# Layer 3's convolution on quarters of the array: sixteen strips in four groups, each product on half the rows and half the columns

## The chip, the cores and the metric

The kernel runs on one core of a Trainium2 chip. The metric is the device time of one execution in microseconds. TensorE is written PE in the profile, VectorE DVE, ScalarE ACT, GpSimd POOL and SyncE SP.

## What is computed

Sixteen samples of 16 channels, 256 x 256 pixels in float32, pass four residual layers. In each, the sample is normalised over pairs of channels, convolved, and added to what came in. Layer 0 is a circular 3x3 convolution, layer 1 a diagonal one of five taps, layer 2 works in the Fourier domain. Only layer 3 is changed:

```python
x_q = jnp.round(jnp.clip(x_cl / scale_input, -n, n))        # n = 127, one scale for the whole tensor
acc = lax.conv_general_dilated(x_q, w_hwio, window_strides=(1, 1), padding=((1, 1), (1, 1)), ...)
out = acc * (scale_input * scale_weight) + bias
...
x = x + _L3_conv_ref(_gn(x), L3_conv_weight_int8, L3_conv_scale_weight, L3_conv_bias)
```

Its input is quantized to whole numbers from -127 to 127, which bf16 holds exactly, convolved with a 3x3 kernel with zeros around the image, scaled and added to x.

## The kernel before

The layers run one after the other: layers 0 and 1 up to about 1270 us, the Fourier stages of layer 2 up to 4046 us, then layer 3 to the end. Between stages the data lie in DRAM: x2d after layer 1, x3d after layer 2.

Layer 3 is the last block of `layers` (from line 1206). An image is cut into S = 8 strips of R = 32 rows. Partition c * 8 + s holds channel c of strip s (`by_strip`, line 253), so a sample is one tile `xt` of [128, 32, 256] float32. A product contracts over all 128 partitions, that is over 16 channels and 8 strips at once. Its weights are a 128 x 128 matrix that is nonzero only where the strip of the input and that of the output agree (`strip_weights`, line 212, which multiplies the 16 x 16 taps with a table of strips). A tap that looks over a strip's edge reads the first or last row of the same tile with a second set of weights, 3 for above and 3 for below, that shifts by one strip; where there is no neighbour they are zero, which gives the padding.

For each sample b (line 1212) the block does this:

- Four chunks of RC = 8 rows: SyncE issues a load of 1 MB (line 1217) from x3d. ScalarE scales and shifts it into u (line 1219; a3 and b3 are the normalisation and the quantizing scale for each partition). VectorE rounds u in place by adding and subtracting a large constant (line 1220), and clips it into the bf16 tile q (line 1221), whose rows have 260 columns, 2 and 2 of them zero for the padding. Two such tiles take turns, `qs`.
- Sixteen tiles of two output rows, t = 1 to 15 and then 0 (`conv`, line 234): nine taps into one PSUM bank [128, 2, 256]. A tap is one product of 512 columns, or two of 256 where its rows lie on both sides of the strip's edge. Line 250 is the product.
- For each tile `done` (line 1223) lets ScalarE scale and shift the bank into o (line 1225), VectorE adds o to xt in place (`tt`, line 189), and after every fourth tile GpSimd issues a store of a chunk of 8 rows, 1 MB, to the output (line 1231).

The pools have 3 tiles of xt, 3 of u, 4 of o and 6 PSUM banks. No order is written by hand in this block: the scheduler of the tile framework puts each engine's instructions into a queue by data flow and its own estimates, and adds the semaphore waits. So loads and quantizing of sample b+1 are mixed with evictions of sample b on ScalarE and VectorE. SyncE issues loads only, and its load of a sample waits until the stores of the sample three before have landed. GpSimd in this block issues stores only. The weights `wt` and the zero columns of `qs` are made during layer 2 (lines 1160 to 1164).

Three other places matter for reading the trace. Line 1142 loads `ot`, 64 partitions a time, the two partition halves in turn, with runs of 1 KB; line 1149 loads `xt` of layer 2 on all 128 partitions with the same runs. In layers 0 and 1, line 370 loads x to 32 partitions a time, and line 466 stores x2d from 32 partitions a time. Line 412 is layer 0's product on column halves of the array.

Of the kernel before, what the change touches and what calls it, by code (L numbers as in the profile page):

```python
# [49 lines left out]
F32 = mybir.dt.float32  # L50
BF16 = mybir.dt.bfloat16
AF = mybir.ActivationFunctionType
ALU = mybir.AluOpType
AX = mybir.AxisListType
PSUM = bass.MemoryType.PSUM
DRAM = bass.MemoryType.DRAM

P = 128
C = 16
S = 8  # L60
R = 32
RC = 8
N = 256
NX = 129
NP = 4
# [6 lines left out]
def constants():  # L72

    n = np.arange(N)
    m = np.arange(128)
    even, odd = 2 * np.arange(64), 2 * np.arange(64) + 1
    fx = np.concatenate([[128], even, odd])
    fy = np.stack([np.concatenate([even, odd]), -np.concatenate([[128], even[1:], odd])], 1).reshape(-1)

    def cos(a, b):  # L80
        return np.cos(2.0 * np.pi * (np.outer(a, b) % N) / N)

    def sin(a, b):
# [12 lines left out]
    inv = np.stack([np.stack([np.concatenate([cos(even, m), v * cos([128], m), v * sin(even[1:], m)], 0),  # L96
                              np.concatenate([cos(odd, m), v * sin(odd, m)], 0)], 1) for v in (-1, 1)], 2)

    h = 0.5 / N**2
    last = np.stack([h * np.concatenate([cos([0], m), 2 * cos(even[1:], m), cos([128], m), -2 * sin(even[1:], m)], 0),  # L100
                     h * np.concatenate([2 * cos(odd, m), -2 * sin(odd, m)], 0)], 1)
    p = np.arange(P)[:, None]
    q = np.arange(P)[None, :]
    c16, c8 = np.arange(C)[None, :], np.arange(S)[None, :]
    s = p % S
    strip = np.stack([s == c8, (s + 1) % S == c8, (s - 1) % S == c8, s + 1 == c8, s - 1 == c8], 1)
# [8 lines left out]
    parts = {  # L115
        "y1": np.concatenate(y1, 1), "x1": np.concatenate(x1, 1), "x2": np.concatenate(x2, 1),
        "full": full, "inv": inv, "last": last, "alone": alone,
        "not0": 1.0 * (p > 0),
        "strip": strip,
        "chan": p // S == c16,  # L120
        "imag": 1.0 * (p % 2 == 1), "real": 1.0 * (p % 2 == 0),
        "group4": (p % 32 // 4 == q % 32 // 4) / 16.0,
        "first": p == 4 * c8,
        "mod": p % 8 == c8,


        "turn": np.stack([np.where(p < 64, 1.0, -1.0), np.where(p // 32 % 2 == 0, -1.0, 1.0),
                          1.0 * (p // 32 % 2 == 1), 1.0 * (p // 32 % 2 == 0)], 1),

        "turn_q": np.concatenate([np.where(im, sb, -sa), np.where(im, -sa, -sb)], 1),  # L130
        "vi": 1.0 * ((p // 64 == np.arange(16)[None, :] // 8) & (p % 8 == np.arange(16)[None, :] % 8)),
        "diag": p // NP % C == c16,
        "m1": np.diag(np.where(p[:, 0] < 64, 1.0, -1.0)) / (2 * N) ** 2,
        "m2": (p == (q + 64) % P) / (2 * N) ** 2,
        "eye": 1.0 * (p == q),
        "mean": np.full((P, P), 1.0 / P),
        "ones": np.ones((P, P)),
        "quarter": np.where(p < 64, 0.25, 0.0),
        "sign": np.where(p < 64, 1.0, -1.0),
        "nat": nat.reshape(128, 2),  # L140
    }
# [23 lines left out]
def layers(ctx, tc, x, w0, w1, w3, sw, bias, ty, tx, p1a, p1b, p1c, p2a, p2b, p2c, resa, resb,  # L165
           const, rows, out):
    nc = tc.nc
# [44 lines left out]
    def strip_weights(pool, src, taps, dtype, name, parts):  # L212
# [2 lines left out]
        raw = pool.tile([P, taps, C], F32, tag=f"{name}r", name=f"{name}r")  # L215
        nc.sync.dma_start(raw, src)
        n = sum(c for _, _, c, _ in parts)
        w = pool.tile([P, n, P], dtype, tag=name, name=name)
        for to, frm, count, m in parts:
            for i in range(count):  # L220
                tt(Q, w[:, to + i, :].rearrange("p (o s) -> p o s", s=S), bc(raw[:, frm + i, :], 2, S),
                   bc(strip[:, m, :], 1, C), MUL)
        return w

    def taps3x3(w, flip):

        taps = []
        for dy in (0, -1, 1):
            for dx in (0, -1, 1):
                ky, kx = (1 - dy, 1 - dx) if flip else (1 + dy, 1 + dx)  # L230
                far = None if dy == 0 else w[:, (9 if dy < 0 else 12) + kx, :]
                taps.append((dy, dx, w[:, 3 * ky + kx, :], far))
        return taps

    def conv(psum, v, taps, done):

        for t in (*range(1, R // 2), 0):
            ps = psum.tile([P, 2, N], F32, tag="ps_c", name="ps_c")
            work = []
            for dy, dx, near, far in taps:  # L240
                cols = slice(2 + dx, 2 + dx + N)
                r0 = 2 * t + dy
                if 0 <= r0 and r0 + 2 <= R:
                    work.append((ps, near, v[:, r0 : r0 + 2, cols]))
                    continue
                for r in range(2):
                    inside = 0 <= r0 + r < R
                    work.append((ps[:, r, :], near if inside else far, v[:, (r0 + r) % R, cols]))
            for i, (o, w, src) in enumerate(work):
                nc.tensor.matmul(o, lhsT=w, rhs=src, start=i == 0, stop=i == len(work) - 1)  # L250
            done(t, ps)

    def by_strip(d):
        return d.rearrange("c (s r) w -> (c s) r w", s=S)


    SL = 32
# [771 lines left out]
    qs = [last_.tile([P, R, 260], BF16, tag=f"q{k}", name=f"q{k}") for k in range(2)]  # L1029


    with ExitStack() as es:
# [97 lines left out]
        with tc.manual_schedule(engines={mybir.EngineType.PE}):  # L1130
            before = None
            exps = exponentials(0)
            for k in range(0, C, 2):
                for b in range(B):
# [23 lines left out]
                        along_x(*before)  # L1158
                    before = (b, k, zts, fs, exps[1], xt)
                    if k == C // 2 and b == 0:  # L1160
                        wt = strip_weights(last_, w3, 9, BF16, "wt3", [(0, 0, 9, 0), (9, 0, 3, 3), (12, 6, 3, 4)])
                        for q in qs:
                            Q.memset(q[:, :, 0:2], 0.0)
                            Q.memset(q[:, :, 258:260], 0.0)
                exps = coming
            along_x(*before)

# [35 lines left out]
        tt(V, so, so, top_all, MUL)  # L1203


    with ExitStack() as es:
        xp = es.enter_context(tc.tile_pool(name="e_x", bufs=3))
        up = es.enter_context(tc.tile_pool(name="e_u", bufs=3))
        rp = es.enter_context(tc.tile_pool(name="e_r", bufs=4))
        ps_c = es.enter_context(tc.tile_pool(name="e_ps", bufs=6, space=PSUM))  # L1210
        taps = taps3x3(wt, False)
        for b in range(B):
            xt = xp.tile([P, R, N], F32, tag="xt4", name=f"xt4_{b}")
            q = qs[b % 2]
            for r in range(0, R, RC):
                rr = slice(r, r + RC)
                nc.sync.dma_start(xt[:, rr, :], by_strip(x3d[b])[:, rr, :])
                u = up.tile([P, RC, N], F32, tag="u", name="u")
                nc.scalar.activation(u, xt[:, rr, :], AF.Identity, bias=b3[:, b : b + 1], scale=a3[:, b : b + 1])  # L1219
                V.tensor_scalar(u, u, ROUND, ROUND, ADD, SUB)  # L1220
                V.tensor_scalar(q[:, rr, 2 : 2 + N], u, 127.0, -127.0, ALU.min, ALU.max)  # L1221

            def done(t, ps):
                o = rp.tile([P, 2, N], F32, tag="o", name="o")
                nc.scalar.activation(o, ps, AF.Identity, bias=bi, scale=so)
                xr = xt[:, 2 * t : 2 * t + 2, :]
                tt(V, xr, xr, o, ADD)
                if t == 0 or (2 * t + 2) % RC == 0 and t >= RC // 2:
                    r0 = 2 * t // RC * RC
                    rr = slice(r0, r0 + RC)  # L1230
                    Q.dma_start(by_strip(out[b])[:, rr, :], xt[:, rr, :])  # L1231

            conv(ps_c, q, taps, done)


def laid_out(inputs):
# [3 lines left out]
        return v.transpose(v.ndim - 1, *axes)  # L1240

    def per_strip(a):
        return np.repeat(np.ascontiguousarray(a).reshape(C, -1), S, axis=0)

    def halves(a):

# [76 lines left out]
```

## Time and profile before

| | |
|---|---|
| median of 3 runs | 4584.78 us (4583.23 to 4585.52) |
| the profiled execution's own time | 4583.97 us |
| its span, first to last instruction | 4582.1 us |
| granted TensorE clock, mean | 0.967 |
| busy in the span: PE, DVE, ACT, POOL | 4195.0, 3004.4, 2706.6, 2165.4 us |
| layer 3: first load issued, first product, last store landed | 4058.0, 4068.2, 4578.2 us |
| layer 3, 4068 to 4582 us: PE, DVE, ACT, POOL busy | 503.3, 313.4, 312.7, 49.4 us |
| layer 3: moved by DMA, mean share of the 16 DMA engines | 255 GB/s, 0.63 |

A group line of the profile reads: source line, engine, operation, what is written and read, shapes, count, then busy time in us, mean of one in ns, and the idle time of the engine just before such instructions with what ended it. Busy time counts overlapping instructions once; the mean of one includes the latency of a pipelined product. A row of the table of stretches gives a stretch in us, its length, busy time and count of PE, of PE's weight loads, DVE, ACT and POOL, then the granted clock, the DMA share and GB/s. The lines themselves stand in the prediction.

### The profile page before, as it was taken

To read this page: it belongs to the slowest core of one execution; us is meant where nothing else is said; L and a number is where in the kernel's file an instruction comes from. 1 tells how busy PE (TensorE), PEld (TensorE's weight loads), DVE (VectorE), ACT (ScalarE), POOL (GpSimd) and SP (SyncE) were. 2 spreads that over 40 slices of the span, in tenths; PEclk is the share of its full clock that TensorE was granted. 3 is DMA by queue.
4 is the path that set the end of the run, shared out by engine and by line. 5 is a ranking of instruction groups with operands and counts; after the bars stand their busy time and mean duration, and the time that the engine had idled before them with its cause. 6 is when DMAs were issued, how large, how long until landed. Compare 5 with 4: busy or idle time off the path is not lost. (4 is left out here: it accounts for less than half of the span.)

```text
span 4582.1 us, 117992 instructions
## 1 busy us (share of the span) xinstructions
PE 4195.0 (92%) x48400; PEld 3115.9 (68%) x48400; DVE 3004.4 (66%) x5682; ACT 2706.6 (59%) x3699; POOL 2165.4 (47%) x3434
## 2 busy tenths in 40 slices
PE   5999999999849998999899999997899999969999
PEld 2555555555529998999777777776788888834444
DVE  4767666767578787777655555544666666676664
ACT  3776768686524443444488888875444444446664
POOL 2242323233336555555566666655777777721000
PEclk9999999999979999999999999998999999989999
DMA  6676767676334444445377777777878788756674
GB/s 150 153 184 151 187 152 189 144 191 150 103 102 155 144 158 144 153 144 166 94 159 170 169 169 169 168 169 208 217 219 218 222 231 233 210 234 252 272 285 175
DMA packets 414939, 820.26 MB, mean 179 GB/s; under 512 B 41600, under 2 KB 306816, under 8 KB 382592
## 3 DMA queue, kind: packets, MB, share of 16 engines
q1 hardware_dynamic: 357056, 577.54, 48.2%
q0 software_dynamic: 57344, 235.18, 16.2%
q8 instruction: 382, 6.26, 0.6%
q14 instruction: 157, 1.29, 0.1%
HBM read 408.86 MB, written 336.07 MB: 163 GB/s over the span
## 5 line engine op out<-in xcount | busy, mean ns | idle before, releaser
L412 PE MATMUL ps<-va,wt 128*64 128x512 f32 (+1 forms) x1632 | 668.6, 571 | 11.4 <-POOL va L384 9.2
L412 PE MATMUL ps<-vb,wt 128*64 128x512 f32 (+1 forms) x1632 | 666.6, 570 | 4.6 <-DMA vb<-va 4.6
L908 ACT COPY sk<-ps_s 64x516 f32<-64x516 f32 x1016 | 593.0, 584 | 114.6 <-PE ps_s L903 95.2
L801 ACT ACTIVATE y<-ps_y,bc 128x384 f32<-128x384 f32 x512 | 297.1, 581 | 421.5 <-PE ps_y L799 421.5
L903 PE MATMUL ps_s<-t,l 128*128 128x258 f32 x2048 | 521.8, 397 | 17.0 <-ACT sk L908 8.3
L250 PE MATMUL ps_c<-q,wt 128*128 128x512 bf16 (+1 forms) x2400 | 503.3, 372 | 17.4 <-DVE q L1221 17.4
L433 ACT ACTIVATE v<-xt,nm 32x2048 f32<-32x2048 f32 x248 | 497.2, 2005 | 9.7 <-PE ps L447 3.5
L189 DVE TENSOR_TENSOR ob<-ps_m,other 128x256 f32<-128x256 f32 x512 | 270.9, 606 | 350.5 <-ACT other L996 346.1
L447 PE MATMUL ps<-v,w1s 128*64 128x259 f32 x4096 | 483.9, 396 | 11.0 <-DVE v L431 6.7
L903 PEld LDWEIGHTS ps_s<-t,l 128*128 128x128 f32 x2048 | 371.4, 191 | 92.2 <-ACT sk L908 8.6
L447 PEld LDWEIGHTS ps<-v,w1s 128*64 128x64 f32 x4096 | 337.5, 141 | 134.6 <-issue 24.6
L250 PEld LDWEIGHTS <-wt 128*128 128x128 bf16 x2400 | 232.8, 97 | 287.8 <-issue 19.8
L412 PEld LDWEIGHTS ps<-va,wt 128*64 128x64 f32 x1632 | 223.0, 137 | 298.6 <-issue 271.5
L1110 PE MATMUL ps_o<-exp,fs 128*128 128x128 f32 x2048 | 402.8, 279 | 18.0 <-ACT fs L1156 18.0
L1109 PE MATMUL ps_o<-c_last,zt 128*128 128x128 f32 x2048 | 401.6, 278 | 0.3
L1109 PEld LDWEIGHTS ps_o<-c_last,zt 128*128 128x128 f32 x2048 | 326.7, 195 | 62.5 <-issue 61.6
L971 PEld LDWEIGHTS ps_m<-z,sk 128*32 128x32 f32 x16384 | 254.4, 110 | 126.8 <-issue 105.8
L971 PE MATMUL ps_m<-z,sk 128*32 128x64 f32 x16384 | 303.8, 222 | 37.0 <-issue 33.2
L189 POOL TENSOR_TENSOR w<-rq 128x512 f32<-128x512 f32 x256 | 320.9, 1280 | 26.6 <-ACT rq L1111 23.8
L189 POOL TENSOR_TENSOR acc<-acc,prod 128x256 f32<-128x256 f32 x240 | 230.1, 959 | 214.4 <-DVE prod L189 208.0
L1110 PEld LDWEIGHTS ps_o<-exp,fs 128*128 128x128 f32 x2048 | 317.1, 195 | 19.0 <-ACT fs L1156 19.0
L796 PE MATMUL ps_y<-c_y,qd 128*128 128x128 f32 x2048 | 315.0, 277 | 5.5 <-ACT y L801 5.5
(341 smaller groups left out, 8699.3 us busy)
## 6 DMA issues: line engine op xcount, KB each, us to landing
xt<-x2d SPq DMA_DIRECT2D x256, 512.0 KB, 4.3
z<-alphad SPq DMA_DIRECT2D x516, 129.0 KB, 4.8
xt<-in_x_dram SPq DMA_DIRECT2D x256, 256.0 KB, 7.6
x2d<-x2s POOLq DMA_DIRECT2D x256, 256.0 KB, 5.0
mixd<-ob SPq DMA_DIRECT2D x128, 512.0 KB, 5.8
ot<-mixd SPq DMA_DIRECT2D x256, 256.0 KB, 7.1
x3d<-xt POOLq DMA_DIRECT2D x128, 512.0 KB, 5.8
xt<-x3d SPq DMA_DIRECT2D x64, 1024.0 KB, 8.9
```

The source lines that it names most:

```text
L189: eng.tensor_tensor(o, a, b, op)
L250: nc.tensor.matmul(o, lhsT=w, rhs=src, start=i == 0, stop=i == len(work) - 1)
L412: nc.tensor.matmul(ps[halves[h], lo:hi, :], lhsT=wt0[:, w, :], rhs=v[:, 2 * t + lo : 2 * t + hi, j : j + N], start=j == 0 and k == 0, stop ...
L433: nc.scalar.activation(to, o.xt[c][q_], AF.Identity, bias=o.g.nm[q_, 1:2])
L447: nc.tensor.matmul(ps[halves[h], k, 0:U], lhsT=o.w1[:, w : w + 64], rhs=v1[:, lo : lo + U], start=first_, stop=not first_)
L796: nc.tensor.matmul(to[:, :, a, :], lhsT=v[:, c, a, i % 2, :], start=a == 0, stop=a == 1, rhs=y1[:, a].rearrange("p (r f) -> p r f", r=2))
L801: nc.scalar.activation(y[:, c, :], ps[:, 0 : 3 * P], AF.Copy, scale=bc2[:, b, i // 2, 0:1])
L903: nc.tensor.matmul(ps[:, d, 0 : 2 * NX], lhsT=ls[h][:, k + d - k0], rhs=t2[:, h, k + d].rearrange("p x r -> p (x r)"), start=True, stop=True)
L908: copy(sks[2 * e8 + n][64 * h : 64 * h + 64, :, 2 * k : 2 * k + 4] .rearrange("p x (k r) -> p x k r", r=2), ps[64 * n : 64 * n + 64, :, 0 ...
L971: nc.tensor.matmul(to, lhsT=sk[:, x_], rhs=z[:, :, x_], start=True, stop=True)
L1109: nc.tensor.matmul(ps[:, a, c, :], lhsT=zts[d][:, a, c, :], rhs=last[:, c, :], start=True, stop=False)
L1110: nc.tensor.matmul(ps[:, a, c, :], lhsT=fs[:, d, a, :], rhs=ey[:, d, c, :], start=False, stop=True)
```

## The change

An image is now cut into 16 strips of 16 rows. Four of them, with 16 channels, make a group of 64 partitions, and there are four groups: image row block s (of 64 rows) has a strip in each group g = 0 to 3. Group n is named by a pair (a, h): its products use row half h of the array, so its quantized input lies on partition half h, and column half a, so its output and its x lie on partition half a. The pairs are (0, 0), (1, 0), (1, 1) and (0, 1). Groups 0 and 2 stay on their half; groups 1 and 3 have a unlike h, and their data change partition halves when they are quantized. In the second chunk of four that a sample has (`moved`), ScalarE makes this move while it scales, in four instructions instead of one; in the other three chunks VectorE makes it while it clips, in four instructions instead of one.

A tile of output is [128, 2, 2, 256] in two PSUM banks, bank h for row half h; there are 4 such tiles (8 banks) and 8 of them a sample instead of 16. For each tap four products follow one another, one for each group, in the order 0, 2, 1, 3. The weights are 64 columns wide and stand on both partition halves. Where a tap looks over the strip's edge, the neighbour is another group: if it lies on the same input half it is read there, otherwise its edge row comes from a small tile qh of [128, 2, 260], which GpSimd fills with four copies a sample across the halves. The first and last group use the shifted weights.

Chunks have 4 rows in each of the two groups on a partition. Each load and each store of a chunk is cut in two, one for each partition half (a = 0 and 1), 512 KB each, with runs of 4 KB instead of 8 KB. ScalarE's and VectorE's instructions on outputs are twice as long and half as many.

The core of the diff:

```diff
-S = 8
-R = 32
-RC = 8
+S = 4
+R = 16
+RC = 4
...
-        w = pool.tile([P, n, P], dtype, tag=name, name=name)
+        w = pool.tile([P, n, C * S], dtype, tag=name, name=name)
...
-        ps_c = es.enter_context(tc.tile_pool(name="e_ps", bufs=6, space=PSUM))
-        taps = taps3x3(wt, False)
+        hp = es.enter_context(tc.tile_pool(name="e_h", bufs=2))
+        ps_c = es.enter_context(tc.tile_pool(name="e_ps", bufs=4, space=PSUM))
+        half = [slice(0, 64), slice(64, P)]
+        groups = ((0, 0), (1, 0), (1, 1), (0, 1))
+
+        def of_half(d, a, rr):
+            g = slice(1, 3) if a else slice(0, 4, 3)
+            return d.rearrange("c (s g r) w -> (c s) g r w", g=4, r=R)[:, g, rr, :]
+
+        def conv(q, qh, t):
+
+            ps = ps_c.tile([P, 2, 2, N], F32, tag="ps_c", name="ps_c")
+            work = [[], [], [], []]
+            for dy in (0, -1, 1):
+                for dx in (0, -1, 1):
+                    near = 3 * (1 + dy) + 1 + dx
+                    cols = slice(2 + dx, 2 + dx + N)
+                    r0 = 2 * t + dy
+                    for n, (a, h) in enumerate(groups):
+                        o = ps[half[a], h]
+                        if 0 <= r0 and r0 + 2 <= R:
+                            work[n].append((h, o, near, q[half[h], a, r0 : r0 + 2, cols]))
+                            continue
+                        for r in range(2):
+                            if 0 <= r0 + r < R:
+                                work[n].append((h, o[:, r], near, q[half[h], a, r0 + r, cols]))
+                            elif n ^ 1 == n + dy:
+                                work[n].append((h, o[:, r], near, q[half[h], 1 - a, (r0 + r) % R, cols]))
+                            else:
+                                w = near if 0 <= n + dy < 4 else (9 if dy < 0 else 12) + 1 + dx
+                                work[n].append((h, o[:, r], w, qh[half[h], int(dy > 0), cols]))
+            for i in range(len(work[0])):
+                for h, o, w, src in (work[n][i] for n in (0, 2, 1, 3)):
+                    nc.tensor.matmul(o, lhsT=wt[half[h], w, :], rhs=src, start=i == 0, stop=i == len(work[0]) - 1)
+            return ps
+
         for b in range(B):
-            xt = xp.tile([P, R, N], F32, tag="xt4", name=f"xt4_{b}")
+            xt = xp.tile([P, 2, R, N], F32, tag="xt4", name=f"xt4_{b}")
             q = qs[b % 2]
             for r in range(0, R, RC):
                 rr = slice(r, r + RC)
-                nc.sync.dma_start(xt[:, rr, :], by_strip(x3d[b])[:, rr, :])
-                u = up.tile([P, RC, N], F32, tag="u", name="u")
-                nc.scalar.activation(u, xt[:, rr, :], AF.Identity, bias=b3[:, b : b + 1], scale=a3[:, b : b + 1])
+                for a in range(2):
+                    nc.sync.dma_start(xt[half[a], :, rr, :], of_half(x3d[b], a, rr))
+                u = up.tile([P, 2, RC, N], F32, tag="u", name="u")
+                moved = r == RC
+                for a, h in groups if moved else ():
+                    nc.scalar.activation(u[half[h], a], xt[half[a], h, rr, :], AF.Identity,
+                                         bias=b3[half[a], b : b + 1], scale=a3[half[a], b : b + 1])
+                if not moved:
+                    nc.scalar.activation(u, xt[:, :, rr, :], AF.Identity, bias=b3[:, b : b + 1], scale=a3[:, b : b + 1])
                 V.tensor_scalar(u, u, ROUND, ROUND, ADD, SUB)
-                V.tensor_scalar(q[:, rr, 2 : 2 + N], u, 127.0, -127.0, ALU.min, ALU.max)
-
-            def done(t, ps):
-                o = rp.tile([P, 2, N], F32, tag="o", name="o")
+                if moved:
+                    V.tensor_scalar(q[:, :, rr, 2 : 2 + N], u, 127.0, -127.0, ALU.min, ALU.max)
+                for a, h in () if moved else groups:
+                    V.tensor_scalar(q[half[h], a, rr, 2 : 2 + N], u[half[a], h], 127.0, -127.0, ALU.min, ALU.max)
+            qh = hp.tile([P, 2, 260], BF16, tag="qh", name="qh")
+            for h, k, a, r in ((0, 0, 0, R - 1), (0, 1, 1, 0), (1, 0, 1, R - 1), (1, 1, 0, 0)):
+                Q.tensor_copy(qh[half[h], k], q[half[1 - h], a, r])
+            for t in (*range(1, R // 2), 0):
+                ps = conv(q, qh, t)
+                o = rp.tile([P, 2, 2, N], F32, tag="o", name="o")
                 nc.scalar.activation(o, ps, AF.Identity, bias=bi, scale=so)
-                xr = xt[:, 2 * t : 2 * t + 2, :]
+                xr = xt[:, :, 2 * t : 2 * t + 2, :]
                 tt(V, xr, xr, o, ADD)
-                if t == 0 or (2 * t + 2) % RC == 0 and t >= RC // 2:
+                if t == 0 or t > 1 and t % 2:
                     r0 = 2 * t // RC * RC
                     rr = slice(r0, r0 + RC)
-                    Q.dma_start(by_strip(out[b])[:, rr, :], xt[:, rr, :])
-
-            conv(ps_c, q, taps, done)
+                    for a in range(2):
+                        Q.dma_start(of_half(out[b], a, rr), xt[half[a], :, rr, :])
```

More of the change, by code (lines that the diff above doesn't have):

```diff
@@ L103, in constants @@
     q = np.arange(P)[None, :]
[L104 removed]
+    c16, c8, c4 = np.arange(C)[None, :], np.arange(8)[None, :], np.arange(S)[None, :]
     s = p % S
[L106 removed]
+    strip = np.stack([s == c4, s + 1 == c4, s - 1 == c4], 1)
     nat = (n + 128) % N - 128
@@ L119, in constants @@
         "strip": strip,
-        "chan": p // S == c16,
+        "chan": p % 64 // S == c16,
         "imag": 1.0 * (p % 2 == 1), "real": 1.0 * (p % 2 == 0),
@@ L223, in strip_weights @@
         return w
[L225 to L254, printed above, removed]
     SL = 32
@@ L1028, in layers @@
     b3 = last_.tile([P, B], F32, tag="b3", name="b3")
-    qs = [last_.tile([P, R, 260], BF16, tag=f"q{k}", name=f"q{k}") for k in range(2)]
+    qs = [last_.tile([P, 2, R, 260], BF16, tag=f"q{k}", name=f"q{k}") for k in range(2)]
     with ExitStack() as es:
@@ L1160, in layers @@
                     if k == C // 2 and b == 0:
-                        wt = strip_weights(last_, w3, 9, BF16, "wt3", [(0, 0, 9, 0), (9, 0, 3, 3), (12, 6, 3, 4)])
+                        wt = strip_weights(last_, w3, 9, BF16, "wt3", [(0, 0, 9, 0), (9, 0, 3, 1), (12, 6, 3, 2)])
                         for q in qs:
-                            Q.memset(q[:, :, 0:2], 0.0)
-                            Q.memset(q[:, :, 258:260], 0.0)
+                            Q.memset(q[:, :, :, 0:2], 0.0)
+                            Q.memset(q[:, :, :, 258:260], 0.0)
                 exps = coming
@@ L1242, in per_strip @@
     def per_strip(a):
-        return np.repeat(np.ascontiguousarray(a).reshape(C, -1), S, axis=0)
+        return np.tile(np.repeat(np.ascontiguousarray(a).reshape(C, -1), S, axis=0), (2, 1))
     def halves(a):
```

## The prediction

> **What bounds the kernel now.** I read the page first, then the chain of work that ended last in order of time, the groups of instructions from 4040 us on, SyncE's own waits, and a table of stretches. Only layer 3 (from 4046 us) is touched. On the page its products are one row, and the chain of waits holds them in one piece:
>
> ```profile
> L250 PE MATMUL ps_c<-q,wt 128*128 128x512 bf16 (+1 forms) x2400 | 503.3, 372 | 17.4 <-DVE q L1221 17.4
> ```
>
> ```profile
> 4057.97 4.80 DMA xt<-x3d
> 4063.42 2.10 ACT u L1219
> 4065.54 1.24 DVE u L1220
> 4066.81 1.24 DVE q L1221
> 4068.18 415.17 PE ps_c L250 x1977
> ```
>
> TensorE starts at 4068.2 us and is busy 503.3 us to 4571.4; before its first product it waited 17.4 us, and for nothing after. So TensorE sets the end here, and the other engines wait for it:
>
> ```profile
> L1225 ACT ACTIVATE o<-ps_c,bi,so 128x512 f32<-128x512 f32 x256 | 195.1, 776 | 186.5 <-PE ps_c L250 186.4
> L189 DVE TENSOR_TENSOR xt<-xt,o 128x512 f32<-128x512 f32 x256 | 173.5, 688 | 155.8 <-ACT o L1225 155.6
> L1219 ACT ACTIVATE u<-xt,b,a 128x2048 f32<-128x2048 f32 x64 | 133.7, 2090 | 17.4 <-DMA xt<-x3d 17.2
> L1220 DVE TENSOR_SCALAR u<-u 128x2048 f32<-128x2048 f32 x64 | 78.3, 1223 | 41.0 <-ACT u L1219 40.9
> L1221 DVE TENSOR_SCALAR q<-u 128x2048 bf16<-128x2048 f32 x64 | 77.1, 1222 | 2.2 <-PE ps_c L250 2.1
> L1231 POOL DMA_DIRECT2D out_dram<-xt x64 | 49.4, 771 | 469.0 <-DVE xt L189 329.6 <-DMA xt<-x3d 139.4
> ```
>
> ScalarE's idle time ends with ps_c, VectorE's with o. The next limit is DMA, and it depends on how many partitions a transfer spans. In the table of stretches the last three columns are the granted clock, the DMA share and GB/s:
>
> ```profile
> 4068.00:4582.00 514.00, 503.34 (x2400) 232.76 (x2400) 313.40 (x383) 312.67 (x318) 49.36 (x64) 0.99 0.63 255
> 4062.00:4087.00 25.00, 18.82 (x80) 8.13 (x81) 19.78 (x21) 20.83 (x15) 0.00 (x0) 0.81 1.01 420
> 3111.00:3125.00 14.00, 3.94 (x48) 2.54 (x48) 5.73 (x13) 13.88 (x22) 5.07 (x4) 0.50 1.13 232
> 3128.00:3131.50 3.50, 3.37 (x22) 1.49 (x26) 1.14 (x1) 1.99 (x5) 2.39 (x2) 0.50 1.10 348
> 10.00:30.00 20.00, 0.00 (x0) 0.00 (x0) 9.34 (x16) 0.00 (x0) 0.00 (x0) 1.00 1.13 216
> ...
> 403.00:409.00 6.00, 6.00 (x46) 3.81 (x44) 3.76 (x8) 5.92 (x4) 3.91 (x10) 1.00 0.99 274
> ...
> 562.00:568.00 6.00, 6.00 (x31) 2.64 (x28) 4.93 (x11) 5.92 (x4) 0.00 (x0) 1.00 0.99 302
> ...
> 852.00:869.00 17.00, 17.00 (x102) 8.93 (x100) 12.51 (x26) 16.77 (x10) 6.81 (x18) 0.98 0.98 250
> ```
>
> Row 1 is layer 3, with DMA a third idle. Row 2: this layer's own loads, 128 partitions with 8 KB runs, 420 GB/s. Row 3: loads of ot, 64 partitions a time, the halves in turn, 1 KB runs: 232. Row 4: 128 partitions with the same 1 KB runs: 348. So it is the 64 partitions that cost, not the short runs. Row 5: 32 partitions, 216. Rows 6 to 8: 32-partition loads of x beside 32-partition stores of x2d.
>
> [...]This trace shows column halves alone: layer 0's pairs of 512-column float32 products start 2 ns apart, a pair every 429 ns, while 258 columns on the full array take 216 ns each (512 would take 429). Row halves it doesn't show.[...]
>
> **The change, part by part.**
>
> *Products.* A tile of output becomes [128, 2, 2, 256], 8 a sample, each 9 taps x 4 products of 512 columns; with the split edges 6 x 36 + 2 x 48 = 312 a sample, 4992 in all against 2400. The trace's start-to-start time of a 512-column bf16 product is 216 ns, 109 for 256. Four at once: per sample 6 x 9 x 216 + 2 x (6 x 216 + 6 x 110) = 15.6 us, 249 us in all.[...] If row halves took turns: 498. I take 249, ends 249 and 498. Weight loads take 97 ns for 128 columns; four tiles of 32 columns go through TensorE every 56 ns in this trace (L971), so loads and issue hide beside 216 ns.
>
> *ScalarE.* Two forms of the same instruction give 0.85 us per 1024 elements: (2090 - 776) / 1536. o: 128 x 1.21 = 155 (was 199). u: 48 x 2.09 = 100, and the moved quarter 16 x 4 x 1.24 = 79 (was 134). Sum 334, as before.
>
> *VectorE.* The sum xt+o: 128 x 1.22 = 156[...]. Rounding unchanged, 78. Clipping: 16 x 1.22 + 48 x 4 x 0.69 = 152 (was 78)[...]. Sum 386. No row shows a VectorE instruction that changes partition halves: at half rate 96 of them cost 0.53 more each, 437 in all[...]. I take 386, or 24.2 us a sample.
>
> *GpSimd.* 64 copies of edge rows; the nearest row is L435's copy of 64x264 at 459 ns: 29 us. Stores double to 128, 98 us at 0.77 each. Queued behind a copy that waits for the last quantized row of sample b+1 stand stores of sample b; who waits for those is SyncE, for the xt buffer. SyncE issues 128 loads instead of 64 at about 0.5 us: hidden behind 2.3 us of transfer each. An edge copy is late only for tiles 7 and 0; six tiles (11.7 us) lie before. All of this I cost at nothing to 2 us a sample, and take 0.5, 8 us in all, together with load queues that run dry while the last store lands.
>
> *Transfers.* Same 67.1 MB in and 67.1 MB out, but every transfer spans 64 partitions, 512 KB, runs of 4 KB. This is the step that decides. At 420 GB/s they need 320 us; one direction at a time at 231, 581 us. Nine saturated stretches of layers 0 and 1 with loads beside stores (three are shown) have 250 to 302 GB/s, mean 271. Those loads have 1 KB runs; full-width transfers gain a factor 420/348 = 1.21 from long ones. So between 271[...] and 327 (the whole factor); I take the middle, R = 299.
>
> *Sum.* Loads flow from 4060 us. Three quarters of sample 0 are in at 4073.9; quantizing (6), tile 3 (2), eviction, add and issue (4.5) bring the first store to 4086.5. Until then 26.5 us x 231 = 6.1 MB are loaded. Both directions then need 2 x 61.0 MB / 299 = 408 us, to 4494.5. The last 6.1 MB of stores, alone, take 27 us; hand-overs 8; a landing 1.5; the close of the program 3.9 (last store landed at 4578.2 of 4582.1). That gives a span of 4535 us against 4582.1, or 47 less. The profiled execution took 4583.97, 1.9 more than its span, and the median of the runs is 0.8 above that: 4535 + 2.7 = about 4538 us.
>
> That both directions overlap is argued: SyncE now waits 387.9 us for stores, since three buffers are full,
>
> ```profile
> SPq L1217 <- DMA out_dram<-xt: 387.9, 26, 36.3
> ```
>
> and when DMA takes 28 us a sample against VectorE's 24, stores queue up while loads run. What is late next is DMA, not TensorE.
>
> **Rivals.** *A, DMA with overlap* (R 262 to 340): 4127 + 122,000/R, so 4486 to 4593 in span; likeliest. *B, compute bound*: halves of opposite directions don't disturb one another, R above 340. Then VectorE's 386 us from 4066.6 plus 9 us of store and close give 4462, with 4% of stalls 4478 in span[...].[...] Against it: the 250 to 302 above. *C, the slower one[...]*. [...]R sinks to 231, and 4127 + 528 = 4655, 73 us more. It decides from R = 268 down, where 4127 + 455 = 4582. For it: the 250 GB/s in the longest stretch. Against: the mean of 271 even at short runs. *D, row halves take turns* (the change doesn't do what it says): TensorE 498 us, about 4580.
>
> **Chances.** A 0.54, B 0.16, C 0.25, D 0.05. About 0.2% (9 us) is what a measurement of this kernel can tell from no change. Faster by more needs R above 274: all of B and about 0.45 of A, 0.61. Within 0.2% (R 263 to 274, and D): 0.13. Slower: 0.26. The range takes A whole, B with its stalls, and C as far as R = 238: 4475 to 4640 us. A's own range is 4489 to 4596.
>
> **What would show it.** Right: DMA share near 1 in the steady part at 260 to 340 GB/s, products waiting for q, ScalarE for xt; four product starts within some ns and 216 ns to the next four; ScalarE near 334 us, VectorE near 386. Loads alone at 4062 to 4085 should run at about 231 GB/s[...]. Stores and loads that alternate, each near 231, show C. Clips of two groups near 1.2 us instead of 0.69 show the half rate.

## The result, and the profile after: no measurable change, with TensorE no longer the bound

The changed kernel takes 4587.27 us (median of 12 runs, 4574.78 to 4590.66) beside 4589.89 us for the kernel before on the same chip (12 runs, 4578.53 to 4594.84): ratio 0.9991, 95% interval 0.9981 to 1.0001. The forecast was 4538 us. The profiled execution took 4588.10 us, with a span of 4586.3.

First the groups of instructions from 4035 us on, one shape to a row; they answer to the rows shown of before (in the changed kernel the product is L1217, the eviction o L1245, scaling L1230 and L1233, rounding L1234, clips L1236 and L1238, edge copies L1241, stores L1252):

```profile
L1217 PE MATMUL ps_c<-q,wt 64*64 64x512 bf16 x4224 | 290.6, 421 | 207.1 <-ACT o L1245 179.2 <-DVE q L1238 24.8 <-DVE q L1236 2.9
L189 DVE TENSOR_TENSOR xt<-xt,o 128x1024 f32<-128x1024 f32 x128 | 158.4, 1250 | 31.9 <-ACT o L1245 30.5
L1245 ACT ACTIVATE o<-ps_c,bi,so 128x1024 f32<-128x1024 f32 x128 | 148.9, 1196 | 10.7 <-DVE xt L189 5.3 <-PE ps_c L1217 4.4
L1238 DVE TENSOR_SCALAR q<-u 64x1024 bf16<-64x1024 f32 x192 | 136.2, 709 | 5.0
L1233 ACT ACTIVATE u<-xt,b,a 128x2048 f32<-128x2048 f32 x48 | 100.4, 2092 | 179.6 <-DMA xt<-x3d 175.9 <-DVE q L1238 1.9 <-DVE q L1236 1.5
L1252 POOL DMA_DIRECT2D out_dram<-xt x128 | 87.4, 687 | 231.6 <-DVE xt L189 176.9 <-DMA xt<-x3d 51.9 <-issue 2.3
...
L1241 POOL COPY qh<-q 64x260 bf16<-64x260 bf16 x64 | 71.2, 1122 | 121.9 <-DVE q L1238 121.6
```

The cause of the old bound is gone: 64x64 products hold TensorE busy for some 306 us instead of 503. An eviction, here and below, is ScalarE's instruction that scales a full PSUM tile into o and so frees the tile. In the idle column two waits of almost the same size have come in: TensorE waits 179.2 us for evictions (all its PSUM tiles are full), and ScalarE, which evicts, waits 175.9 us for loads before a scaling. The row of the stretch that layer 3 fills (busy us of PE, PEld, DVE, ACT and POOL, then granted clock, DMA share, GB/s) shows that no engine is full:

```profile
4068.00:4582.00 514.00, 305.60 (x4992) 185.75 (x4992) 385.83 (x400) 321.54 (x240) 158.47 (x192) 0.85 0.88 261
```

VectorE, the busiest, works 386 of 514 us, and 261 GB/s is hardly more than the 255 of before. The chain of work that ended last, which before held one piece of 415 us of products, is now broken up; this is one of its sections (start, duration, what):

```profile
4247.16 7.24 DMA out_dram<-xt
4255.20 7.13 DMA xt<-x3d
...
4265.52 1.23 ACT u L1230
...
4288.56 7.20 DMA xt<-x3d
4295.87 2.10 ACT u L1233
4300.43 1.24 ACT u L1230
...
4321.64 7.15 DMA xt<-x3d
```

A load every 33 us (4255.2, 4288.6, 4321.6), with scaling between. ScalarE's timeline shows what stands there (start, duration; in brackets the idle time ahead and what ended it):

```profile
4295.87 2.09 ACT L1233 ACTIVATE u<-xt,b,a 128x2048 f32<-128x2048 f32 x1 [11.44 <-DMA xt<-x3d]
4297.87 1.19 ACT L1245 ACTIVATE o<-ps_c,bi,so 128x1024 f32<-128x1024 f32 x1
4299.18 2.49 ACT L1230 ACTIVATE u<-xt,b,a 64x1024 f32<-64x1024 f32 x2
4301.69 1.21 ACT L1245 ACTIVATE o<-ps_c,bi,so 128x1024 f32<-128x1024 f32 x1
...
4313.26 4.47 ACT L1245 ACTIVATE o<-ps_c,bi,so 128x1024 f32<-128x1024 f32 x4
4328.90 2.09 ACT L1233 ACTIVATE u<-xt,b,a 128x2048 f32<-128x2048 f32 x1 [11.17 <-DMA xt<-x3d]
```

Evictions o stand behind scalings u in ScalarE's queue, and here none went ahead of a scaling that waited: the products before had ended by 4290.90, ScalarE sat idle for 11.44 us until the load of the u at 4295.87 was there, the eviction behind that u starts at 4297.87, and TensorE, after 8.20 us without work, goes on at 4299.10. And the load waits for stores. Issue and landing of single transfers, from the trace's DMA records, close the circle (us):

```
last two stores of a sample     issued 4280.28, landed 4287.79
first load into that buffer     issued 4287.93, chunk 0 complete 4295.76
u of that chunk                 4295.87, other evictions queued behind it
stores of those evictions       issued 4300.65 to 4313.75, landed by 4320.88
first load into that buffer     issued 4321.02   (33.1 us after the one before)
```

With three whole-sample buffers, a load of sample b+2 goes into the buffer of b-1, once the last store of b-1 has landed. Read off the order of ScalarE's instructions, the scalings of b+2 stand behind the fourth, fifth, seventh and eighth of the eight evictions of b. (The expectations call the last place the first eviction of b+1; it is just ahead of that.) So half of b's evictions, and the stores that they feed, wait for the stores of b-1. That is a loop of two transfers' latency and some ScalarE work per sample. Its slack is the number of evictions between the last store that frees a buffer and the scaling that needs the load into it: four. I call this the **loop theory**.

It also forces the directions apart. I sorted the packets of layer 3 by which direction moved over 20 GB/s, averaged over 1 us (us @ GB/s; the last column is neither; the experiments' rows are explained below):

```
                   loads alone   stores alone  both          none
before             165 @ 391     200 @ 313      18 @ 405     142
after              165 @ 211     154 @ 231     172 @ 371      40
before, half width 158 @ 213     144 @ 228     187 @ 363      41
after, 4 buffers   131 @ 213     122 @ 247     208 @ 367      33
far order          214 @ 217     156 @ 271     116 @ 389      41
near order          51 @ 217      65 @ 243     298 @ 357       6
near, full width   120 @ 335     113 @ 332     138 @ 409      40
before, near       167 @ 384     198 @ 315      20 @ 378     143
```

One direction over 64 partitions gets 211 to 231 GB/s, as forecast. Loads beside stores get 371, more than the 299 I had assumed. But they run beside each other for a third of the time only. ScalarE's order had the same loop before (the scalings of b+2 stood behind the sixth, seventh, ninth and tenth of the sixteen evictions of b); at full width and with TensorE needing 31 us a sample, it cost nothing. The row of before doesn't show it, though: its directions keep apart as much with the scalings moved back (last row).

### The profile page after: what moved, and what is told of

It is laid out like the page before. It is cut to its first block, busy times and chain, and to the rows that moved or that the text cites. A ratio compares the mean times of both kernels' runs of the same rounds, so it can differ in the third digit from the quotient of the medians.

```text
span 4586.3 us, 123297 instructions
## 1 busy us (share of the span) xinstructions
PE 4004.8 (87%) x50992; PEld 3081.6 (67%) x50992; DVE 3077.3 (67%) x5698; ACT 2708.7 (59%) x3619; POOL 2270.4 (50%) x3562
## 5 line engine op out<-in xcount | busy, mean ns | idle before, releaser
L1217 PE MATMUL ps_c<-q,wt 64*64 64x512 bf16 (+1 forms) x4800 | 305.6, 403 | 207.1 <-ACT o L1245 179.2
L1217 PEld LDWEIGHTS <-wt 64*64 64x64 bf16 x4992 | 185.7, 115 | 326.8 <-issue 264.2
```

What stands on the lines that cost most here:

```text
L1217: nc.tensor.matmul(o, lhsT=wt[half[h], w, :], rhs=src, start=i == 0, stop=i == len(work[0]) - 1)
```

## Experiments

Rivals to the loop theory: the **port theory** (the half-width transfers don't carry more; "port" is only a name, no run shows one), and the **compute theory** (hand-overs between engines set 33 us a sample, whatever the transfers do). Ratios are to the kernel before, measured beside it on the same chip.

### Full-width transfers in the changed kernel

```diff
-                for a in range(2):
-                    nc.sync.dma_start(xt[half[a], :, rr, :], of_half(x3d[b], a, rr))
+                nc.sync.dma_start(xt[:, :, rr, :], of_all(x3d[b], rr))
...
-                    for a in range(2):
-                        Q.dma_start(of_half(out[b], a, rr), xt[half[a], :, rr, :])
+                    Q.dma_start(of_all(out[b], rr), xt[:, :, rr, :])
```

> The changed kernel with its loads and stores of layer 3 on all 128 partitions again, 1 MB each with runs of 4 KB. The strips then hold other pixels than the products assume, so the output of layer 3 is that of a scrambled image; every instruction on the engines stays. Loop theory (ScalarE takes the evictions of sample b behind the quantizing of sample b+2, whose load waits for the stores of sample b-1, so each sample pays one chain of store landing, load, quantizing, eviction, and half-width transfers stretch its legs): the legs halve, VectorE's 386 us become the bound, about 4500 us. Port theory (64 partitions give 261 GB/s on average whatever the order): 320 us of transfers, VectorE bound too, about 4500. Compute theory (the new order of work on the engines takes 33 us a sample by itself): stays at 4587.

Measured: 4638.12 us, ratio 1.0113 (1.0097 to 1.0128): slower, and outside what any theory had expected.

```profile
L1235 ACT ACTIVATE u<-xt,b,a 128x2048 f32<-128x2048 f32 x48 | 100.2, 2090 | 240.1 <-DMA xt<-x3d 235.7 <-DVE q L1240 2.3 <-issue 1.8
```

ScalarE's wait for loads grew from 176 to 236 us although the first load into a freed buffer was sooner there: issued at 4307.64, its scaling began at 4312.88, 5.2 us later, against 7.9 us in the changed kernel (4287.93 to 4295.87). The order on ScalarE had moved with the edit: the scalings of b+2 now stood after the second to fifth eviction of b, two to three places earlier. The slack was two evictions in place of four. The experiment changed two things; a later one (near order, full width) parts them.

### Four sample buffers

```diff
-        xp = es.enter_context(tc.tile_pool(name="e_x", bufs=3))
-        up = es.enter_context(tc.tile_pool(name="e_u", bufs=3))
-        rp = es.enter_context(tc.tile_pool(name="e_r", bufs=4))
+        xp = es.enter_context(tc.tile_pool(name="e_x", bufs=4))
+        up = es.enter_context(tc.tile_pool(name="e_u", bufs=2))
+        rp = es.enter_context(tc.tile_pool(name="e_r", bufs=3))
```

> The changed kernel with four whole xt buffers instead of three; to make room, 2 tiles of u instead of 3 and 3 of o instead of 4. The load of sample b+2 then waits for the stores of sample b-2, which are long done. Loop theory: the chain is cut, loads and stores lie beside each other at the 371 GB/s that they reach where both run (22.6 us a sample), VectorE's 24 us a sample bound it: 4500 to 4530 us. Port theory: no change, 4587. Compute theory: no change, 4587.

Measured: 4552.42 us, ratio 0.9926 (0.9911 to 0.9941). The direction is right, the size was not: some 30 us below the changed kernel (the ratios 0.9926 and 0.9991), with 57 to 87 expected.

```profile
L1233 ACT ACTIVATE u<-xt,b,a 128x2048 f32<-128x2048 f32 x48 | 100.5, 2093 | 136.4 <-DVE q L1238 86.8 <-issue 28.0 <-DMA xt<-x3d 21.1
```

The wait for loads fell from 176 to 21 us; but most of the idle time stayed, and now the clips end it, which free one of only two scaled tiles. The smaller pool by itself was tried as a control:

```diff
-        up = es.enter_context(tc.tile_pool(name="e_u", bufs=3))
+        up = es.enter_context(tc.tile_pool(name="e_u", bufs=2))
```

> The control of the run with four sample buffers: the kernel after with two scaled tiles in place of three and nothing else; the order on ScalarE stays that of the kernel after. Loop theory and theory that buffers of samples are what count: 4580 to 4600, as the kernel after. If the smaller pool itself had helped, it would fall to about 4552.

Measured: 4580.27 us, ratio 0.9991 (0.9984 to 0.9997), as the changed kernel. So the gain came with the fourth buffer, not from the smaller pool. But ScalarE's order had moved here too: the scaling of b+2 now began behind the seventh eviction of b-1, five places earlier, while the load that it needs waited for the stores of b-2. That is a slack of seven.

### Twelve chunk-sized buffers in place of three whole ones

```diff
-            xt = xp.tile([P, 2, R, N], F32, tag="xt4", name=f"xt4_{b}")
+            xts = [xp.tile([P, 2, RC, N], F32, tag="xt4", name=f"xt4_{b}_{r}") for r in range(R // RC)]
```

> The changed kernel with xt cut into 12 tiles of one chunk (4 rows in each of two groups), the same memory as three whole buffers. A load then waits for the store of one chunk and not for those of a whole sample. Loop theory: the chain loses the wait for the last of eight stores and becomes shorter by some 5 to 8 us a sample until VectorE binds: 4500 to 4540 us. Port theory and compute theory: no change, 4587.

Measured: 4598.16 us, ratio 1.0025 (1.0016 to 1.0034): a miss. The load of a chunk now waits for one chunk's store, but ScalarE's order had moved again: it scaled b+3 in place of b+2, behind the seventh and eighth eviction of b and the third and fourth of b+1. The slots come free at the third, fifth, seventh and eighth eviction of b, so if they are filled again in that order, the slack is three to four evictions, no more than before (ScalarE waited 118 and 53 us for loads at its two scaling lines). That is argued; this order wasn't held fixed with chunk buffers.

### Half-width transfers in the kernel before

```diff
-                nc.sync.dma_start(xt[:, rr, :], by_strip(x3d[b])[:, rr, :])
+                for p in (slice(0, 64), slice(64, P)):
+                    nc.sync.dma_start(xt[p, rr, :], by_strip(x3d[b])[p, rr, :])
...
-                    Q.dma_start(by_strip(out[b])[:, rr, :], xt[:, rr, :])
+                    for p in (slice(0, 64), slice(64, P)):
+                        Q.dma_start(by_strip(out[b])[p, rr, :], xt[p, rr, :])
```

> The kernel before with each load and store of layer 3 cut into two of 64 partitions, 512 KB, runs of 8 KB; nothing else. Loop theory: TensorE's 31.4 us a sample hide part of the longer chain; 10 to 40 us slower than before, 4600 to 4630. Port theory: 134.2 MB at 261 GB/s are 514 us after 27 us of loads alone, about 4605 to 4615. Compute theory: transfers don't matter, 4590.

Measured: 4591.79 us, ratio 1.0011 (1.0002 to 1.0019): no cost to speak of. The 142 us in which neither direction moved shrank to 41; TensorE still set the end. Only the compute theory had this number, though for the kernel before it says no more than that the products hide the transfers. The run doesn't test the width alone, as ScalarE's order moved with the edit: the scalings of b+2 began behind the tenth or eleventh of sixteen evictions of b in place of the sixth, which loosens the loop.

### The order written out: near, far, and half-way

The strong test of the loop leaves transfers, buffers and operations alone and changes where the scaling stands. In all of the following, the queues of ScalarE, VectorE, TensorE and GpSimd in layer 3 are written out by hand, as the core of this edit shows; scale, clip and edges hold the unchanged lines for one chunk or sample.

```diff
+        es.enter_context(tc.manual_schedule(engines={
+            mybir.EngineType.PE, mybir.EngineType.DVE, mybir.EngineType.Activation, mybir.EngineType.Pool}))
...
+        for s in range(B):
+            for c in range(R // RC):
+                todo.setdefault(max(0, T * (s - 1) + (1, 3, 5, 7)[c]) if s else 0, []).append((0, s, c))
+                todo.setdefault(max(0, T * (s - 1) + (2, 4, 6, 8)[c]) if s else 0, []).append((1, s, c))
...
+                if i == T - 1 and b + 3 < B:
+                    load(b + 3)
+                quantize(T * b + i + 1)
```

The first tuple says after how many evictions of s-1 the scalings of s stand, the second the same of rounding and clips.

> Only the order in layer 3 differs from the kernel after: on ScalarE, VectorE, TensorE and GpSimd it is written out by hand, so that the scaling of the next sample (b+1) stands between the evictions of sample b, one chunk after every second of them, in place of the scaling of the sample after next (b+2), whose loads wait for stores that the evictions queued behind it feed. Buffers, transfers and operations are those of the kernel after. Loop theory (load, scaling, evictions and stores chained through ScalarE's queue): the scaling then waits for loads that were issued a sample earlier, loads and stores overlap, and a sample takes what the slower of VectorE (24 us) and the two transfers at 371 GB/s (22.6 us) takes, 25 to 29 us in place of 32 to 33: 4490 to 4540 us; ScalarE's wait for loads falls from 176 to under 60 us. Port theory (the half-width transfers carry no more): no change, 4580 to 4595. Compute theory (the hand-overs between engines set the pace): no change or slower, since the quantizing now stands nearer to the products that need it, 4590 to 4650.

Measured: **4483.03 us**, ratio 0.9774 (0.9761 to 0.9787), a little better than the loop theory's range. The waits of the near order in layer 3 (what waits, for what; us, times, longest):

```profile
ACT u L1239 <- DMA xt<-x3d: 80.8, 18, 14.7
PE ps_c L1217 <- DVE q L1247: 59.2, 74, 19.6
...
PE ps_c L1217 <- ACT o L1274: 25.8, 17, 4.0
```

```profile
4068.00:4475.00 407.00, 304.87 (x4968) 181.75 (x4967) 376.44 (x394) 309.28 (x235) 189.80 (x192) 0.93 0.97 322
```

TensorE's wait for evictions fell from 179 to 26 us. ScalarE still waits 81 us for loads (the expectation said under 60): 18 of these before 4110 us, then some 21 in every 100 us, 6.3 at most at a time where the changed kernel had over 11. DMA share is 0.97, at 322 GB/s; both directions move together for 298 us instead of 172. VectorE is busy 376 of 407 us. In the steady part ScalarE's queue alternates, two evictions and a scaling:

```profile
4284.42 2.30 ACT L1274 ACTIVATE o<-ps_c,bi,so 128x1024 f32<-128x1024 f32 x2
4286.61 2.09 ACT L1239 ACTIVATE u<-xt,b,a 128x2048 f32<-128x2048 f32 x1
4288.60 2.30 ACT L1274 ACTIVATE o<-ps_c,bi,so 128x1024 f32<-128x1024 f32 x2
4290.77 2.10 ACT L1239 ACTIVATE u<-xt,b,a 128x2048 f32<-128x2048 f32 x1
```

The control has the places of the changed kernel: (-4, -3, -1, 0) for the scalings, which is behind the fourth, fifth, seventh and eighth eviction of s-2, and (0, 0, 2, 4) for the clips.

> The control of the hand-written order: written out in the same way, but with each sample's scaling at the places that it has in the kernel after (sample b+2 after the fourth, fifth and seventh eviction of b and the first of b+1). All theories: within 0.5% of the kernel after, 4565 to 4610 us; loop theory adds that ScalarE again waits over 140 us for loads. A time near 4520 would mean that the hand-written form, and not the place of the scaling, made the difference.

Measured: 4594.93 us, ratio 1.0018 (1.0008 to 1.0028). Writing the order by hand gains nothing; the place of the quantizing is worth 112 us.

```profile
PE ps_c L1217 <- ACT o L1274: 168.7, 42, 17.8
ACT u L1239 <- DMA xt<-x3d: 92.9, 19, 14.6
ACT u L1239 <- DVE q L1247: 75.6, 14, 5.7
```

TensorE's wait for evictions is back at 169 us. The figure of over 140 us of waiting for loads was missed: 92.9 (and 13.6 at the other scaling line), since another 75.6 ended with clips that freed a scaled tile. So in the control ScalarE's queue is held up in two ways, and only one of them is the loop through the transfers; the run with five scaled tiles below has that one nearly alone. In between, (-2, 0, 2, 4) and (0, 2, 4, 6):

> The hand-written order with the scaling half-way between the far and the near one: sample b+2 after the sixth eviction of b and after the next sample's own start, second and fourth. Loop theory: the chain from the last store of b-1 to the first store that depends on it shrinks by degrees, so the time lies between near and far, 4505 to 4560. If only the sample that is scaled mattered (b+2 or b+1), and not how many evictions stand behind it, it would equal one of the two ends, 4483 or 4595.

Measured: 4536.39 us, ratio 0.9893 (0.9880 to 0.9907). The time follows the slack by degrees: 4595, 4536 and 4483 us for four, six and nine evictions (in the near order, the scaling of b+1 behind the first eviction of b needs the stores of b-2). The traces show the same for layer 3 alone, from its first load's issue to its last store's landing: 525, 471 and 423 us (518 in the changed kernel). Slack isn't the whole of it: the run with four sample buffers had a slack of seven and 4552 us, more than the half-way order with six, with waits for scaled tiles in place of waits for loads.

Near, half-way and far differ in the clips' and edge copies' places too. One more run parts that (the reverse, scaling near and clips far, can't be written, since a clip follows its scaling): ScalarE far, the rest near, (-4, -3, -1, 0) and (2, 4, 6, 8), with five scaled tiles.

> ScalarE far, the rest near: the scaling of sample b+2 stands where it does in the kernel after and in the far control (after the fourth, fifth and seventh eviction of b and the first of b+1), while rounding, clips and edge copies on VectorE and GpSimd stand where they do in the near order. Five scaled tiles in place of three hold what lies between; buffers of samples and all work are the same. Near and far so far differed on VectorE and GpSimd too, where adds and stores could queue behind clips and edge copies. Theory that ScalarE's queue carries the loop: as the far control, 4575 to 4600. Rival, that the place of the clips and edge copies made the difference: as the near order, 4480 to 4500.

Measured: 4636.98 us, ratio 1.0108 (1.0091 to 1.0124).

```profile
ACT u L1239 <- DMA xt<-x3d: 210.0, 23, 15.0
PE ps_c L1217 <- ACT o L1274: 183.4, 38, 17.6
DVE xt L189 <- ACT o L1274: 153.9, 28, 16.1
```

The rival (near clips make the gain) is out: with ScalarE far, nothing is gained. The time is 37 us above what the loop theory said, so the place of the clips and edge copies, or the five tiles, is not neutral. A reading that fits, not tested alone: the later clips stand ahead of the last adds of a sample on VectorE, the last stores leave later, and the loop grows by that.

### Near order with full width, with four buffers, and with the old layout

Full width, with the transfer lines of the first experiment:

> The near order with every load and store of layer 3 over all 128 partitions, twice the size and half as many; the strips then stand on other rows of the image, so the output is a scrambled one, while work and bytes are the same. Loop theory: with the loop cut the transfers have slack, so width matters little: within 1% of the near order with half-width transfers, 4480 to 4540 us. Port theory (half-width transfers set the pace): well below the near order at half width, by 50 us or more.

Measured: 4468.46 us, ratio 0.9743 (0.9730 to 0.9755). With the order held, full width gains 15 us over half width (the intervals don't meet), not the 50 of the port theory, and the 4638 of the first experiment was the order's doing. With bufs 4, 2 and 3 as above:

> The near order with a fourth whole sample buffer (scaled tiles 2 in place of 3, eviction tiles 3 in place of 4, to make the space). Loop theory: loads come a further sample early, the wait for them nearly vanishes, and VectorE or the transfers' own rate set the pace: equal to the near order with three buffers or up to 40 us below it, 4460 to 4530. Compute theory: equal to the near order or slower by the smaller pools. Port theory: as the kernel after, less the 35 us that a fourth buffer alone gave.

Measured: 4480.20 us, ratio 0.9767 (0.9754 to 0.9779), no different from the near order with three buffers. So once the scalings stand near, a fourth buffer adds nothing measurable; what it gained in the earlier experiment fits a loosened loop.

Last, the near order in the kernel before, at 2, 6, 10 and 14 of its 16 evictions:

```diff
+                todo.setdefault(max(0, T * (s - 1) + (2, 6, 10, 14)[c]) if s else 0, []).append((0, s, c))
+                todo.setdefault(max(0, T * (s - 1) + (4, 8, 12, 16)[c]) if s else 0, []).append((1, s, c))
```

> The kernel before (8 strips, products over the whole array, 128-partition transfers) with the near order of the earlier experiment: the scaling of sample b+1 stands between the evictions of sample b, one chunk after every fourth of sixteen. It asks what the change is worth where the loop is cut. Theory that the change's gain was there and the loop hid it: the old layout is then held by its products, 498 us of TensorE plus about 25 us ahead of them and after them, so 4565 to 4590, no or little gain; the near order gains some 100 us only with the new layout. Rival, that the order alone is the gain and the layout is worth nothing: 4480 to 4500.

Measured: 4584.29 us, ratio 0.9999 (0.9991 to 1.0007).

```profile
4068.00:4582.00 514.00, 503.80 (x2400) 232.87 (x2400) 321.90 (x384) 316.35 (x319) 40.74 (x64) 0.99 0.64 256
```

TensorE is busy 503.8 of 514 us, as in the kernel before. The order alone gains nothing, the change alone gains nothing, both together gain 2.3%.

## Why the prediction was wrong

- **What bounds the kernel: right.** TensorE set the end, and the change removed that bound. D (row halves take turns) is out: around 4303 us the trace has four products of 64x64x512 starting within 36 ns and the next four 217 ns later, as forecast (216); that they run at once was an estimate until then. (One reading in the prediction was off: most pairs of layer 0's column halves start 52 ns apart, not 2; a pair every 429 ns is right.)
- **TensorE's sum: too low, without effect.** It was busy for 306 us, with 249 forecast. After a wait of 8.2 us, with a granted clock of 0.50 (4299 to 4301 us), fours start 427 ns apart instead of 217 at a clock of 1.00; 81 of the 306 us ran at 0.50. In the near order TensorE is as busy, 305 us, and the gain is there.
- **Sums of VectorE and ScalarE: right.** VectorE 386 us, forecast 386 (the sum xt+o 1250 ns, estimated at 1.22 us; clips 709 ns in the mean, 690 in the median, estimated at 0.69 us; the half rate, supposed at 437 us, didn't come); ScalarE 328 by its groups, forecast 334. The edge copies were mis-sized: 1122 ns, not 459, so 71 us, not 29. That isn't what cost the time: in the near order they take 74 us and the gain is there.
- **Loads alone: right.** 211 GB/s in packets, with 231 forecast.
- **Rate with both directions: too low.** 371 GB/s, outside 271 to 327. By the prediction's own test (R above 340) rival B should have followed, with a span of 4478 us; it was given 0.16. The changed kernel's span was 4586.3, so B was right on the rate and wrong on the time: it left out the loop too. The near order, where the loop is loosened, comes out at 4475.9. That is close to B's figure, but in part by luck: layer 3's first load left 9 us earlier there than in the kernel before, and whether VectorE alone bounds it is open.
- **The failed step: "That both directions overlap is argued".** The sum let both directions run together from the first store on, in 408 us, or 28 us of DMA a sample. I read SyncE's 388 us of waiting for stores as a sign that buffers are full and stores will queue up. The row says only that loads wait for a buffer: it is 388.6 us as well in the kernel before with the near order. In the changed kernel this wait is one leg of a loop: loads wait for stores, scaling waits for loads, evictions wait behind scaling, stores wait for evictions. Once round it takes 33 us a sample, and the prediction had no term for it. "Stores queue up while loads run" held for 172 of 519 us (from the first load's issue to the last store's landing).
- **The time inside the range is luck.** 4587 us lies in 4475 to 4640, and even in A's own range, but A would need R = 265 for it (4127 + 122,000 / 265), and 371 was measured. No change within 0.2% had been given 0.13, for R between 263 and 274 or for D, neither of which came.
- **C looks right and isn't.** It had the directions take turns whatever the program does, with R sunk to 231; that was a guess, and no run shows it. Where both run, 371 GB/s are carried; they take turns because the program makes them, as the near order shows (both for 298 us).
- **"What is late next is DMA" was half right.** ScalarE did wait for xt, as forecast; but a wait that a transfer ends isn't a limit of the transfers' rate: with the same transfers, the near order cut this wait from 176 to 81 us.

Where the gain went: TensorE's freed 200 us became 179 us of waiting for evictions that stood behind scalings in ScalarE's queue. To see it beforehand, the prediction would have had to write down one sample's cycle with the order of ScalarE's queue, and ask how long it is with TensorE at zero. The trace of before held parts of it: 5 us from issue to landing for the first load and 7 for the first store, and ScalarE's instructions in their order, though the scheduler was free to change that order with the edit.

## What to carry to other kernels

When a change frees the bounding engine, don't only add up the next engine's work; walk once round every loop that a reused buffer closes (store, load, first consumer, whatever stands behind it in its queue, store) and compare its length with the new time per step. Instructions that wait for a transfer belong behind work that is ready, or far enough after their transfer's issue: here moving scalings back by five to seven evictions was worth 112 us, more than a fourth buffer (some 30 us) or twice the transfer width (15 us). And an edit to sizes or pools may reorder the queues; compare the orders before giving a difference to the edit.

## What was not expected of the hardware

- Loads beside stores over 64 partitions each ran at 357 to 389 GB/s together, while loads alone got 211 to 217 and stores alone 228 to 271; at full width both got 378 to 409, loads alone 335 to 391, stores alone 313 to 332 (all from the table above). Whether load and store lay on the same half or on opposite ones isn't parted by any run.
- Clips that move data from one partition half to the other took as long as those that stay: in the near order, where their order is known, the medians of the four clips of a chunk are 685 and 691 ns (stay) and 690 and 687 ns (move) for 1024 elements.
- Copies of 64x260 bf16 from one half to the other on GpSimd took 1122 ns in the changed kernel, 1181 in the near order and 723 in the far one, in the mean; single copies took from 0.40 to 1.46 us in each of the three. What sets this is open.
- Still open: which of VectorE (376 of 407 us) and the transfers (share 0.97) bounds the near order. The 15 us at full width, with the share down to 0.84 and VectorE at 379, point to some of both: between 4100 and 4440 us VectorE is busy for 327 of 340 us at half width, with a DMA share of 1.00, and for 332 at full width, with a share of 0.88.
